# Attention inside an adaLN block: short diagonal units merged, and the softmax denominators summed wholly on GpSimd

## The chip, the cores and the metric

The kernel runs on one core of one Trainium2 chip. The metric is the device time of one execution in microseconds (us). Three runs of the kernel before gave 1782.09, 1782.79 and 1783.23 us; their median, 1782.79 us, is the time to compare with.

## What is computed

The reference is one transformer block with adaptive layer norm on a sequence `x` of 2048 rows of 1024 features, all in float32. A modulation vector gives six rows `sa, ca, ga, sb, cb, gb`. Cut to what matters here:

```python
h = layernorm(x) * (1 + ca) + sa
q, k, v = h @ Wq, h @ Wk, h @ Wv          # 32 query heads of 32 features, 8 key/value heads
q, k = rope(q), rope(k)
scores = q @ k.T / sqrt(32)               # each of the 8 k heads serves 4 query heads
scores = where(column > row, -huge, scores)   # causal mask, 2048 x 2048 per head
x = x + ga * ((softmax(scores) @ v) @ Wo)
h = layernorm(x) * (1 + cb) + sb
x = x + gb * lora_experts(h)              # top 1 of 8 experts, each of rank 16
```

The change touches only the attention: the row maxima of the scores, the weights `exp(score - max)`, and their sums (the softmax denominators).

## The kernel before

**Steps.** The attention is done in 32 steps `n = (qb, m)`: query block `qb` of 512 rows (four of them) times a group `m` of four query heads (eight of them). A step of block `qb` has `nk = 4 * (qb + 1)` key tiles of 128 keys: 4, 8, 12 or 16. The last four key tiles of a step lie on the diagonal; key tile `kc` there needs only the queries from `offset(kc) = kc * 128 - qb * 512` on, so that the four have 512, 384, 256 and 128 columns.

**Visits.** TensorE holds a step's work in *visits*. The letters are those of the order that is described below.

- **M, maxima** (`maxima_units`, 320 visits before). For 128 query rows `t` of the block and 512 keys `kc`, four matmuls that run side by side in the four row groups of the array (32 rows each, one per head) write four PSUM banks `sm` (L1426). On the diagonal (`kc == qb`) only `(t + 1) * 128` columns exist, and 16 small bf16 matmuls from the tables `pick` and `later` (L1419) write the mask first. VectorE then takes one maximum per bank (L1432). When a step's last unit is done, `split_maxima` (L1441 to L1447) turns the maxima into three bf16 parts on GpSimd.
- **R, rows** (`shift_rows`, L1454, L1457). The negated maxima are turned into rows `nt`.
- **S, scores** (`Attend.weights`, 320 visits before). For one key tile, again in the four row groups and in four PSUM banks `sc`: the negated maxima by a bf16 matmul (L1479), the mask on the diagonal (L1487, 16 matmuls), the scores (L1492). ScalarE takes the exponential of each bank into the tile `et` (L1498), 128 keys by four heads by 512 queries. There are four `et` buffers.
- **P, sums** (`weighted_sum`, L1508). Four matmuls, in the four *column* groups of the array, add `et` times `v` into one bank `po`. Right after each, `accumulate` (L1524, L1526) adds `et` to the running sum `acc` in SBUF: on GpSimd, and in the last of the 32 steps on VectorE. It covers all key tiles but the last two.
- **D, shares** (`denominators`, L1534). Four column-group matmuls with a matrix of ones sum `acc` over its 128 partitions into the bank `pd`, and eight more do so for the last two key tiles, taken straight from their `et` buffers. ScalarE copies `pd` (L1539), VectorE inverts it in four parts (L1543), GpSimd multiplies (L1547).
- **F and T, everything else** on TensorE: the projections (`pq`, `pk`, `pv`), the output product (`pw`), the second half of the block (`tr_c`, `pa`, `pwh`, `pf`). They are column-group or full-array matmuls.

A visit of kind M or S is in *row form* here, P, D, R and most of F in *column form*.

**What sets the order.** `plan_order` searches, before anything is issued, for an order of all visits. It keeps a list of states, each with the clock that it imagines for each engine, with when each PSUM bank (eight), each `et` buffer and the running sum become free, and with prices in us written into it: a change of form between visits (`start`), 0.00875 us per column for GpSimd's additions, and so on. Each state is ranked by TensorE's idle time so far and by how far maxima and other work are from the pace that they should have. The maxima run about one step ahead of the scores. The order found is then issued as it is; the engines wait for one another only by semaphores. At most two key tiles are scored and not yet summed, the third key tile of a step is not scored before D of the step before, and `acc` is not begun again before that D.

**Start and end.** The first 125 us or so project the first 512 rows. The last 47 us (`finale`) have the last step's D, its part of the output product, and the second half of the last 512 rows.

The functions that the change touches, and what calls them, with the profile's line numbers:

Of the kernel before, what the change touches and what calls it, by code (L numbers as in the profile page):

```python
# [10 lines left out]
F32 = mybir.dt.float32  # L11
# [85 lines left out]
def plan_order(parts, trail, steps, ahead, starts, tiles, ends, rates, gates):  # L97
# [87 lines left out]
    def maxima(s):  # L185
        n, t, kc = ahead[s[MAXIMA]]
        qb = steps[n][0]
        nk = QB if kc < qb else (t + 1) * P
        masked = kc == qb
        ready, turned = take(s, 4), unit_needs[s[MAXIMA]][1]  # L190
        if turned:
            ready = max(ready, s[TURNED][turned - 1] + TO_PE)
        s[PE] = start(s, "Rb" if masked else "R", ready) + 0.00167 * nk + (0.15 if masked else 0.0)
        s[WORK] += 0.00167 * nk
        after = s[PE] + TO_ENGINE
        give(s, *[(use(s, DVE, 0.07 + 0.00104 * nk, after) + TO_PE, b) for b in s[GOT]])
        s[MAXIMA] += 1
        if s[MAXIMA] - 1 == final[n]:
            done = use(s, POOL, 1.3, use(s, DVE, 0.15, 0.0) + BETWEEN)
            s[MINUS] = s[MINUS] + (done + TO_PE,)  # L200
# [10 lines left out]
    def scores(s):  # L211
        n, kc = tiles[s[SCORED]]
        if kc == 0:
            s[NOW] = n
            flush(s)
        width = QB - max(0, kc * P - steps[n][0] * QB)
        s[PE] = start(s, "Rb", max(take(s, 4), s[MINUS][n])) + 0.00209 * width
        s[WORK] += 0.00209 * width
        if kc >= 4 * steps[n][0]:
            s[PE] += 0.13  # L220
        free, s[ETS] = s[ETS][0], s[ETS][1:]
        after = max(s[PE] + TO_ENGINE, free)
        read = []
        for b in s[GOT]:
            done = use(s, ACT, 0.07 + 0.00083 * width, after)
            read.append((done + TO_PE, b))
        give(s, *read)
        s[READY] = s[READY][1:] + (done,)
        s[CREDIT] += rates[s[SCORED]]
        s[SCORED] += 1  # L230
# [4 lines left out]
    def sums(s):  # L235
        i = s[SUMMED]
        n, kc = tiles[i]
        nk = 4 * (steps[n][0] + 1)
        width = QB - max(0, kc * P - steps[n][0] * QB)
        ready = et_ready(s, i)  # L240
        at = ready + TO_PE
        if kc == 0:
            at = max(at, take(s, 1))
            s[SUM_BANK] = s[GOT][0]
        s[PE] = start(s, "C", at) + 0.00167 * width
        s[WORK] += 0.00167 * width
        if kc == nk - 1:
            give(s, (use(s, ACT, 0.5, s[PE] + TO_ENGINE) + TO_PE, s[SUM_BANK]))
        adder, us = (DVE, 0.0043) if n == last_step else (POOL, 0.00875)
        if kc == 1:  # L250
            s[ACC] = use(s, adder, us * QB, max(ready + BETWEEN, s[ACC_FREE]))
            free_et(s, max(s[ACC], s[PE]), 2)
        elif 1 < kc < nk - 2:
            s[ACC] = use(s, adder, us * width, ready + BETWEEN)
            free_et(s, max(s[ACC], s[PE]), 1)
        s[SUMMED] += 1

    def shares(s):
        flush(s)
        n = s[SHARED]  # L260
        ready = max(take(s, 1), s[ACC] + TO_PE, et_ready(s, ends[n] - 1) + TO_PE)
        s[PE] = start(s, "C", ready) + 0.00167 * (QB + 384)
        s[WORK] += 0.00167 * (QB + 384)
        s[ACC_FREE] = s[PE] + TO_ENGINE
        free_et(s, s[PE], 2)
        s[RD] = use(s, ACT, 0.5, s[PE] + TO_ENGINE)
        give(s, (s[RD] + TO_PE, s[GOT][0]))
        s[LATER] = 5
        s[SHARED] += 1
# [57 lines left out]
    def choices(s):  # L327
# [10 lines left out]
        if s[SCORED] < len(tiles):  # L338
            n, kc = tiles[s[SCORED]]
            if n < s[ROWS] and s[SCORED] - s[SUMMED] < 2 and not (s[SHARED] < n and kc > 1):  # L340
                found.append((max(four, s[MINUS][n] - 0.8), "S", scores))
        if s[SUMMED] < s[SCORED]:
            n, kc = tiles[s[SUMMED]]
            if not (s[SHARED] < n and kc == 1) and s[FILL] >= sums_need[s[SUMMED] > 0]:
                found.append((et_ready(s, s[SUMMED]) + TO_PE, "P", sums))
# [22 lines left out]
    for n, kc in tiles:  # L368
        span = starts[n + 2] - starts[n + 1] if n < last_step else 0.0
        due.append(starts[n + 1] + span * (kc + LEAD) / (4 * (steps[n][0] + 1)))  # L370
# [93 lines left out]
def adaln_block_kernel(  # L464
# [937 lines left out]
    def maxima_units(n):  # L1402
# [3 lines left out]
        def unit(t, kc):  # L1406
            nk = QB if kc < qb else (t + 1) * P
# [5 lines left out]
            ps = score_banks(f"sm_{n}_{t}_{kc}")  # L1413

            if masked:
                for s in range(4):
                    o = t * P + s * HD
                    for j, rows in groups:
                        nc.tensor.matmul(  # L1419
                            ps[j][:, o : o + HD], later[rows, s, :],  # L1420
                            pick[rows, s, s * HD : (s + 1) * HD], start=(s == 0), stop=False,
                        )
            spans = [(t * P, nk), (0, t * P)] if masked and t else [(0, nk)]
            for a, b in spans:
                for j, rows in groups:
                    nc.tensor.matmul(  # L1426
                        ps[j][:, a:b], q[rows, t * P : (t + 1) * P],
                        k[rows, kc * QB + a : kc * QB + b], start=not masked,
                        stop=(a, b) == spans[-1],
                    )  # L1430
            for j in range(4):
                nc.vector.tensor_reduce(mx[:, t, j : j + 1, kc], ps[j][:, :nk], AX.X, ALU.max)  # L1432

        units = [lambda t=t, kc=kc: unit(t, kc) for t in range(4) for kc in range(qb + 1)]
        return units

# [22 lines left out]
    class Attend:  # L1459
        def __init__(self, n):  # L1460
            self.n = n
            self.qb, self.m = steps[n]
            self.nk = 4 * (self.qb + 1)
            self.ets = {}

            last = n == len(steps) - 1
            self.adder = nc.vector if last else nc.gpsimd
# [4 lines left out]
        def weights(self, kc):  # L1472

            off, qb = self.offset(kc), self.qb
            q, k, nt = quad(self.m, qb), k_t[:, self.m // 4, :], nts[self.n % 2]
            ps = score_banks(f"sc_{self.n}_{kc}")

            for j, rows in groups:
                nc.tensor.matmul(  # L1479
                    ps[j][:, off:], ones_h[rows, :], nt[rows, off:],  # L1480
                    start=True, stop=False,
                )
            if kc >= 4 * qb:
                for s in range(4):
                    w = (s + 1) * HD
                    for j, rows in groups:
                        nc.tensor.matmul(  # L1487
                            ps[j][:, off : off + w],
                            pick[rows, s, :], later[rows, s, :w], start=False, stop=False,
                        )  # L1490
            for j, rows in groups:
                nc.tensor.matmul(  # L1492
                    ps[j][:, off:], k[rows, kc * P : (kc + 1) * P], q[rows, off:],
                    start=False, stop=True,
                )
            et = epool.tile([P, 4, QB], F32, tag="et", name=f"et_{self.n}_{kc}")
            for j in range(4):
                nc.scalar.activation(  # L1498
                    et[:, j, off:], ps[j][:, off:], AF.Exp, scale=1.0 / math.sqrt(HD)
                )  # L1500
            self.ets[kc] = et

        def weighted_sum(self, kc):
            off, et = self.offset(kc), self.ets[kc]
            if kc == 0:
                self.po = bank(f"po_{self.n}")
            for j, rows in groups:
# [3 lines left out]
                    start=(kc == 0), stop=(kc == self.nk - 1),  # L1511
                )
            if kc == self.nk - 1:
                nc.scalar.copy(quad(self.m, self.qb), self.po)

        def accumulate(self, kc):

            off, et = self.offset(kc), self.ets[kc]
            if kc == 1:
# [5 lines left out]
            elif 1 < kc < self.nk - 2:  # L1525
                self.adder.tensor_add(self.acc[:, :, off:], self.acc[:, :, off:], et[:, :, off:])  # L1526

        def denominators(self):
            pd = bank(f"pd_{self.n}")
            parts = [(0, self.acc)]  # L1530
            parts += [(self.offset(kc), self.ets[kc]) for kc in (self.nk - 2, self.nk - 1)]
            for i, (off, et) in enumerate(parts):
                for j, rows in groups:
                    nc.tensor.matmul(  # L1534
                        pd[rows, off:], ones_p[:, :HD], et[:, j, off:],
                        start=(i == 0), stop=(i == 2),
# [20 lines left out]
    for n, (qb, m) in enumerate(steps):  # L1557
        ahead += [(n, t, kc) for t in range(4) for kc in range(qb + 1)]
# [7 lines left out]
    tiles = [(n, kc) for n in range(len(steps)) for kc in range(4 * (steps[n][0] + 1))]  # L1566
    attend = [Attend(n) for n in range(len(steps))]
    ends = [sum(s.nk for s in attend[: n + 1]) for n in range(len(steps))]
# [23 lines left out]
    for n, t, kc in ahead:  # L1592
        qb, m = steps[n]
        b = 2 * qb + t // 2
# [13 lines left out]
        parts, [k for k, _ in trail], steps, ahead, starts, tiles, ends, rates, gates  # L1608
# [5 lines left out]
    for letter, banks in order:  # L1614
# [15 lines left out]
        elif letter == "S":  # L1630
            n, kc = tiles[i]
            now[0] = n
            attend[n].weights(kc)
        elif letter == "P":
            n, kc = tiles[i]
# [68 lines left out]
```

## Time and profile before

| | value |
|---|---|
| median of three runs | 1782.79 us |
| the profiled execution's own time | 1782.16 us |
| its span, first to last instruction | 1780.4 us |
| granted TensorE clock, mean | 0.996 |
| VectorE busy | 1094.3 us, 61% of the span |
| ScalarE busy | 740.0 us, 42% |
| maxima on VectorE (L1432) | 1280 instructions, 689.0 us |
| exponentials on ScalarE (L1498) | 1280 instructions, 578.4 us |
| additions to `acc` on GpSimd (L1526, 180 instructions, and L1524, 31) | 792.8 and 132.1 us |

TensorE's share in four stretches that are cut where a block's last D begins: 200.1 of 204 us (block 0, from 125 us on), 324.3 of 327 us (block 1), 503.2 of 507 us (block 2) and 568.8 of 570 us (block 3).

How to read the rows: "PE" is a matmul, "PEld" the load of its weights, which may lie under the matmul before. A float32 matmul shows as two records, so that "x8" stands for four matmuls. Matmul ends are modelled and overlap what follows, so the length of a visit is read here from its start to the next visit's start. "32*128" is a row-form matmul (32 rows of the array, 128 columns), "128*32" a column-form one.

### The profile page before, as it was taken

The page shows a single profiled execution, that of the slowest core. Times are in us where ns is not written, and L with a number is a line of the kernel's source. Part 1 is how long each engine was busy: PE and PEld are TensorE (multiplying, and loading weights), DVE is VectorE, ACT ScalarE, POOL GpSimd, SP SyncE. Part 2 cuts the span into 40 slices and gives each one's busy share as a digit, 9 for nine tenths or more (in the row PEclk, how much of TensorE's full clock was granted, in tenths as well). Part 3 has the DMA queues.
Part 4 walks back from the last instruction along what each step waited for, and adds up shares of the span by engine and source line. Part 5 has one row for each costly group of instructions (what it writes and reads, how often), then busy time and mean ns, then how long its engine had stood idle before and what let it go on. Part 6 is the DMA issues. An engine that isn't in the chain of part 4 may idle for free.

```text
span 1780.4 us, 55951 instructions
## 1 busy us (share of the span) xinstructions
PE 1747.0 (98%) x25112; PEld 708.9 (40%) x25112; DVE 1094.3 (61%) x2160; ACT 740.0 (42%) x1634; POOL 1185.1 (67%) x568
## 2 busy tenths in 40 slices
PE   7999999999999999999999999999999999999997
PEld 3655555444444333334444343333333333333333
DVE  2455456755755674676475566575566765666497
ACT  1203334344433424455444333454544444455452
POOL 1233343487567649657885866978979778798852
PEclk9999999999999999999999999999999999999999
DMA  9512323212422421131103011101102111110101
GB/s 350 181 30 74 115 80 103 73 50 62 137 73 96 153 87 49 49 102 61 61 26 125 26 49 68 41 37 49 49 25 73 37 61 49 49 49 25 49 13 49
DMA packets 68496, 130.57 MB, mean 73 GB/s; under 512 B 3744, under 2 KB 20768, under 8 KB 68256
## 3 DMA queue, kind: packets, MB, share of 16 engines
q1 hardware_dynamic: 66928, 125.85, 20.5%
q8 instruction: 196, 3.21, 0.8%
q10 hardware_dynamic: 1328, 1.15, 0.2%
q14 instruction: 44, 0.36, 0.1%
HBM read 118.59 MB, written 8.39 MB: 71 GB/s over the span
## 4 chain that ended last, share of the span: by engine, by line
PE 88%; POOL 6%; DVE 2%; issue 2%; DMA 1%; ACT 1%; POOLq 0%; ACTq 0%; DVEq 0%
PE sm L1426 15%; PE po L1508 14%; PE sc L1492 12%; PE pw L675 11%; PE pq L966 11%; PE sc L1479 5%; POOL acc L1526 5%; PE pd L1534 3%; PE pk L675 3%; PE pv L675 2%; PE pa L675 2%; PE open L966 2%; PE pf L675 2%; PE sm L1419 1%; DVE mx L1432 1%
## 5 line engine op out<-in xcount | busy, mean ns | idle before, releaser
L1432 DVE TENSOR_REDUCE mx<-sm 128x1 f32<-128x512 f32 (+3 forms) x1280 | 689.0, 602 | 397.7 <-PE sm L1426 396.2
L1498 ACT ACTIVATE et<-sc 128x512 f32<-128x512 f32 (+3 forms) x1280 | 578.4, 540 | 705.5 <-PE sc L1492 701.3
L1526 POOL TENSOR_TENSOR acc<-acc,et 128x2048 f32<-128x2048 f32 (+1 forms) x180 | 792.8, 4404 | 31.8 <-ACT et L1498 22.8
L1426 PE MATMUL sm<-k_t,q 32*128 32x512 f32 (+3 forms) x3328 | 336.6, 475 | 3.0 <-ACT et L1498 3.0
L1492 PE MATMUL sc<-q,k_t 32*128 32x512 f32 (+3 forms) x2560 | 297.2, 536 | 0.0
L1508 PE MATMUL po<-et,v_sb 128*32 128x512 f32 (+3 forms) x2560 | 294.8, 538 | 0.1
L675 PE MATMUL pw<-w,q 128*32 128x512 f32 x1920 | 238.7, 598 | 0.0
L1524 POOL TENSOR_TENSOR acc<-et,et 128x2048 f32<-128x2048 f32 (+1 forms) x31 | 132.1, 4261 | 98.5 <-ACT et L1498 83.1
L966 PE MATMUL pq<-h_t,w 128*32 128x256 f32 x3072 | 191.9, 384 | 0.0
L1426 PEld LDWEIGHTS sm<-k_t,q 32*128 32x128 f32 x3328 | 139.5, 184 | 116.9 <-issue 43.5
L966 PEld LDWEIGHTS pq<-h_t,w 128*32 128x32 f32 x3072 | 90.5, 110 | 100.6 <-issue 44.8
L1508 PEld LDWEIGHTS po<-et,v_sb 128*32 128x32 f32 x2560 | 59.0, 108 | 175.5 <-issue 152.3
L1543 DVE RECIPROCAL rd<-rd 128x128 f32<-128x128 f32 x128 | 112.4, 919 | 18.9 <-ACT rd L1539 18.8
L1479 PE MATMUL sc<-nt,ones_h 32*128 32x512 bf16 (+3 forms) x1280 | 120.1, 352 | 3.5 <-ACT rd L1539 2.9
L1112 POOL TENSOR_TENSOR x<-ag,x 128x512 f32<-128x512 f32 x40 | 60.9, 1523 | 87.3 <-DVE ag L1111 87.3
L1492 PEld LDWEIGHTS sc<-q,k_t 32*128 32x128 f32 x2560 | 115.5, 185 | 5.8 <-issue 2.1
L1479 PEld LDWEIGHTS <-ones_h 32*128 32x128 bf16 x1280 | 32.9, 91 | 207.6 <-issue 201.5
L844 POOL TENSOR_TENSOR swap_q<-swap_q,cs 128x512 f32<-128x512 f32 x32 | 40.9, 1277 | 105.7 <-DVE swap_q L841 105.7
L675 PEld LDWEIGHTS pw<-w,q 128*32 128x32 f32 x1920 | 50.1, 109 | 129.3 <-issue 110.8
L1547 POOL TENSOR_TENSOR q<-q,rd 128x512 f32<-128x512 f32 x31 | 41.6, 1343 | 67.3 <-DVE rd L1543 49.5
L1111 DVE TENSOR_TENSOR ag<-pw,gate 128x512 f32<-128x512 f32 x40 | 27.5, 687 | 62.5 <-PE pw L675 60.9
L844 POOL TENSOR_TENSOR swap_k<-swap_k,cs 128x512 f32<-128x512 f32 x8 | 10.2, 1276 | 82.7 <-DVE swap_k L841 82.7
(146 smaller groups left out, 1340.0 us busy)
## 6 DMA issues: line engine op xcount, KB each, us to landing
w<-in_wo_dram SPq DMA_DIRECT2D x112, 256.0 KB
w<-in_wmod_dram SPq DMA_DIRECT2D x48, 512.0 KB
w<-in_wq_dram SPq DMA_DIRECT2D x48, 512.0 KB
x<-in_x_dram SPq DMA_DIRECT2D x32, 512.0 KB
out_dram<-x SPq DMA_DIRECT2D x16, 512.0 KB
w<-in_wv_dram SPq DMA_DIRECT2D x12, 512.0 KB
w<-in_wk_dram SPq DMA_DIRECT2D x12, 512.0 KB
wq<-in_wq_dram SPq DMA_DIRECT2D x8, 512.0 KB
```

The lines of the kernel that those rows point to most:

```text
L675: nc.tensor.matmul(dst[rows], left[:, rows], right, start=start, stop=stop)
L966: nc.tensor.matmul(ps[j * HD : (j + 1) * HD, a * TB : (a + 1) * TB], self.query_weights(half, k, j * P + h * HD), self.h_t[:, k, :], start ...
L1112: nc.gpsimd.tensor_add(x1[t][:, cols], tmp, x1[t][:, cols])
L1426: nc.tensor.matmul(ps[j][:, a:b], q[rows, t * P : (t + 1) * P], k[rows, kc * QB + a : kc * QB + b], start=not masked, stop=(a, b) == spans ...
L1432: nc.vector.tensor_reduce(mx[:, t, j : j + 1, kc], ps[j][:, :nk], AX.X, ALU.max)
L1479: nc.tensor.matmul(ps[j][:, off:], ones_h[rows, :], nt[rows, off:], start=True, stop=False,)
L1492: nc.tensor.matmul(ps[j][:, off:], k[rows, kc * P : (kc + 1) * P], q[rows, off:], start=False, stop=True,)
L1498: nc.scalar.activation(et[:, j, off:], ps[j][:, off:], AF.Exp, scale=1.0 / math.sqrt(HD))
L1508: nc.tensor.matmul(self.po[rows, off:], v_sb[:, kc, 4 * (self.m // 4) + j, :], et[:, j, off:], start=(kc == 0), stop=(kc == self.nk - 1),)
L1524: self.adder.tensor_add(self.acc[:, :, off:], first[:, :, off:], et[:, :, off:])
L1526: self.adder.tensor_add(self.acc[:, :, off:], self.acc[:, :, off:], et[:, :, off:])
L1543: nc.vector.reciprocal(part, part)
```

## The change

Three things change, and the planner is told of each.

1. In the maxima of steps from the third on, the diagonal units of `t = 0` (128 columns) and `t = 2` (384 columns) are one visit in one set of four banks (`unit_list`). The two units' matmuls and VectorE's two maxima per bank stay as many as they were.
2. In the scores, the key tiles of a step are taken in the order ..., nk-3, nk-1, nk-2. Tiles nk-3 (384 columns) and nk-1 (128 columns) are one visit in one set of four banks; it takes two `et` buffers at once.
3. GpSimd adds the last two key tiles to `acc` too, so that D has only the four matmuls over `acc`. The last step keeps D as it was.

```diff
+    def unit_list(n):
+
+        qb = steps[n][0]
+        if n < 2:
+            return [((t,), 0) for t in range(4)]
+        out = []
+        for t in range(4):
+            out += [((t,), kc) for kc in range(qb)]
+            out += [((), ((1,), qb), ((0, 2), qb), ((3,), qb))[t]] if t else []
+        return out
...
             for j in range(4):
-                nc.vector.tensor_reduce(mx[:, t, j : j + 1, kc], ps[j][:, :nk], AX.X, ALU.max)
...
+                for t, a, b in runs:
+                    nc.vector.tensor_reduce(mx[:, t, j : j + 1, kc], ps[j][:, a:b], AX.X, ALU.max)
...
+            self.order = [*range(self.nk - 2), self.nk - 1, self.nk - 2]
+            self.packs = [[kc] for kc in self.order]
+            self.packs[-3:-1] = [self.order[-3:-1]]
...
+            self.apart = 2 if last else 0
...
             for j in range(4):
-                nc.scalar.activation(
-                    et[:, j, off:], ps[j][:, off:], AF.Exp, scale=1.0 / math.sqrt(HD)
-                )
...
+                for kc, off, a, b in runs:
+                    nc.scalar.activation(
+                        self.ets[kc][:, j, off:], ps[j][:, a:b], AF.Exp, scale=1.0 / math.sqrt(HD)
+                    )
...
-            elif 1 < kc < self.nk - 2:
+            elif 1 < i < self.nk - self.apart:
                 self.adder.tensor_add(self.acc[:, :, off:], self.acc[:, :, off:], et[:, :, off:])
...
         def denominators(self):
             pd = bank(f"pd_{self.n}")
             parts = [(0, self.acc)]
-            parts += [(self.offset(kc), self.ets[kc]) for kc in (self.nk - 2, self.nk - 1)]
+            apart = self.order[self.nk - self.apart :]
+            parts += [(self.offset(kc), self.ets[kc]) for kc in apart]
             for i, (off, et) in enumerate(parts):
                 for j, rows in groups:
                     nc.tensor.matmul(
                         pd[rows, off:], ones_p[:, :HD], et[:, j, off:],
-                        start=(i == 0), stop=(i == 2),
+                        start=(i == 0), stop=(i == self.apart),
                     )
```

In the planner, D now waits for `acc` alone, and the buffers of the last two tiles come free when GpSimd has added them, not when D has read them:

```diff
-        elif 1 < kc < nk - 2:
+        elif 1 < kc < (nk - 2 if n == last_step else nk):
             s[ACC] = use(s, adder, us * width, ready + BETWEEN)
             free_et(s, max(s[ACC], s[PE]), 1)
...
-        ready = max(take(s, 1), s[ACC] + TO_PE, et_ready(s, ends[n] - 1) + TO_PE)
-        s[PE] = start(s, "C", ready) + 0.00167 * (QB + 384)
-        s[WORK] += 0.00167 * (QB + 384)
+        s[PE] = start(s, "C", max(take(s, 1), s[ACC] + TO_PE)) + 0.00167 * QB
+        s[WORK] += 0.00167 * QB
         s[ACC_FREE] = s[PE] + TO_ENGINE
-        free_et(s, s[PE], 2)
```

Since the planner searches anew, the whole issue order differs from the third step on.

## The prediction

> **What bounds the kernel now.** I read the page first. TensorE is busy almost throughout, and the chain that ended last is 88% TensorE. GpSimd has 6% of that chain, which needs a closer look, since the change gives it more to do.
>
> ```profile
> span 1780.4 us, 55951 instructions
> PE 1747.0 (98%) x25112; PEld 708.9 (40%) x25112; DVE 1094.3 (61%) x2160; ACT 740.0 (42%) x1634; POOL 1185.1 (67%) x568
> PE   7999999999999999999999999999999999999997
> POOL 1233343487567649657885866978979778798852
> PE 88%; POOL 6%; DVE 2%; issue 2%; DMA 1%; ACT 1%; POOLq 0%; ACTq 0%; DVEq 0%
> ```
>
> Second, who waits for GpSimd's sum: the answer for the tile `acc` has only one waiting line on TensorE's side, 1.8 us in all. Its 6% of the chain is a path that runs beside busy TensorE, not a stall.
>
> ```profile
>   PEld pd L1534: 1.8, 3
> ```
>
> Third, the windows. In block 3 TensorE has 1.2 us without work out of 570, and GpSimd 468 us of work: 82%, its fullest stretch.
>
> ```profile
> 1163.00:1733.00 570.00, 568.81 (x6684) 192.20 (x6680) 372.94 (x661) 281.25 (x598) 467.63 (x161) 1.00 0.12 43
> ```
>
> So time is gained by taking work or form changes off TensorE, and by hardly anything else. Fourth, the timeline of TensorE, for the price of a change of form. The first column is the start; I take a visit from its start to the next one's.
>
> ```profile
> 1147.84 1.06 PE L675 MATMUL pw<-w,q 128*32 128x512 f32 x8
> 1148.84 0.23 PE L1479 MATMUL sc<-nt,ones_h 32*128 32x128 bf16 x4
> ...
> 1151.95 1.04 PE L675 MATMUL pw<-w,q 128*32 128x512 f32 x8
> 1152.81 0.40 PE L1508 MATMUL po<-et,v_sb 128*32 128x128 f32 x8
> ...
> 1160.96 1.03 PE L1492 MATMUL sc<-q,k_t 32*128 32x512 f32 x8
> 1161.82 1.03 PE L1426 MATMUL sm<-k_t,q 32*128 32x512 f32 x8
> 1162.77 1.07 PE L1534 MATMUL pd<-acc,ones_p 128*32 128x512 f32 x8
> 1163.66 0.83 PE L1534 MATMUL pd<-et,ones_p 128*32 128x256 f32 x16
> 1164.42 0.40 PE L1479 MATMUL sc<-nt,ones_h 32*128 32x512 bf16 x4
> ...
> 1182.28 1.03 PE L1492 MATMUL sc<-q,k_t 32*128 32x512 f32 x8
> 1183.24 0.66 PE L742 MATMUL tr_c<-ident,xn 128*128 128x128 f32 x4
> ```
>
> The same four output matmuls take 1.00 us ahead of a row-form visit and 0.86 ahead of another column visit: 0.14 for going in. With `po` it is 1.00 against 0.88 (medians of the whole timeline), with `pq` 0.55 against 0.45. I take 0.12. The scores' four matmuls take 0.86 ahead of another row visit and 0.96 ahead of a full-array one: 0.10 for going out. A run of row-form visits costs 0.22 us beside its own work.
>
> **The change part by part.**
>
> **D without the two last tiles** (31 of 32 steps). The line `pd<-et`, x16, goes from 1163.66 to 1164.42, 0.76 us; 0.12 of that is the change of form, which the matmuls over `acc` pay instead. 0.64 x 31 = 19.8 us of TensorE, all on its path. ScalarE's copy and VectorE's inversions stay.
>
> **Shared visits.** 30 maxima and 32 score visits go. Their matmuls, masks, maxima and exponentials stay, so the gain is the change of form alone, and only where the neighbours are column work. I counted that in both programs' issue orders: before, 320 + 320 visits lie in 588 runs of row form; after, 290 + 288 in 535. 53 x 0.22 = 11.7 us. The rest of the new order pays nothing else: what full-array work adds and loses in changes is under ten in number.
>
> Here the Trainium skill is weighed. *TensorEngine Tiling (Array Packing)*, Key Properties, says that a change of tiling mode drains TensorE; *TensorE: Matmul & The Clock Gate*, Single matmul latency, puts the constant part of a lone matmul at about 175 ns. If each change cost that (an estimate from these pages), a run would cost 0.35 and the 53 runs 18.6 us. The rows have 0.10 to 0.14, so I keep 11.7; 18.6 is the far end.
>
> A shared visit keeps its banks until both halves are done: a bank's first reader starts after the last matmul of the second half, some 0.4 us later. In return a set of four banks is asked for 62 times less. Maxima of 512 columns between column visits have a median of 1.07 us but a mean of 1.11, so bank waits are some 0.04 us each, 13 us over 320; a tenth fewer visits may save 1. I take 1, between -2 (all waits grow by a sixth) and 3.
>
> **GpSimd.** It gains an addition of 4 x 128 and one of 4 x 256 in 31 steps. Its rows: 2048 elements 4541 ns, 1536 elements 3455 ns, 512 elements 1272 to 1343 ns. 1024 lies between: 2.37 us. 1.28 + 2.37 = 3.65 us a step, 113 us in all, 1185 to 1298. In block 3, seven steps are GpSimd's: 468 + 26 = 493 of some 560 us, 88%. That is still cover, but at the handover from one step to the next it is a new wait: D now waits for the additions of the last tiles, and behind D wait the third tile of the next step and the start of its sum. Behind the additions themselves, in GpSimd's own queue, wait the split of the maxima, the rotary products and the additions to `x`.
>
> What is it worth? The handover in the fence above: GpSimd ended its last addition at 1156.1, and D began at 1162.8. All 31 handovers, read so: 20 had more than 3.65 us between, the other eleven fall short by 16 us together. That is the cost if TensorE keeps its old order and stands idle for each shortfall. The new order puts work there: from the scores of the last tile to D, TensorE has 4 to 21 us of other visits (their columns at the rates above), in block 3 from 7 to 17. A sum that is up to date needs 4 x 0.389 us of exponentials, 1.28 and 2.37: 5.2 us. One that is also behind by tile nk-3 needs 8.7. Six to eight steps have less than that, by some 20 us in all. So 0 to 20 us; I take 3, near the lower end, since the row nearest to it (waits of D for `acc`) is 1.8 us today, with an order made the same way. It cannot be below zero: no wait goes away by it.
>
> Again a rule stands against it: *GPSIMD Engine Reference*, Engine selection, would have such additions on VectorE, at half the time. The rows agree on the ratio (VectorE 2.69 us for 2048 elements in the last step), and the pair would take about 1.9 us a step in place of 3.65. By the rule 31 x 1.8 = 54 us are given away. By the windows they are on no path as long as TensorE has work to put in: 0 to 20.
>
> **The two `et` buffers at once.** Of four, a shared visit takes two, and the last tiles' buffers come free after GpSimd, not after D. This holds up scores, not TensorE, while maxima and projections are there; it is in the 0 to 20.
>
> **Sum.** Against the profiled execution, 1782.2 us: - 19.8 - 11.7 - 1 + 3 = 1752.7. The median of the runs is 0.6 above that execution, so 1753 us, 1.7% less. Start (125 us) and end (47 us) have none of this.
>
> **The rivals.**
>
> *GpSimd becomes the bound at the handovers* (5%, the slower side). One mechanism: in blocks 2 and 3 GpSimd is a full addition behind when the last tile comes, and TensorE has used up what it may do before D, so that each of 15 steps waits a full 4.5 us: 68 us, 1753 - 3 + 68 = 1818. It turns into a loss from 31.5 / 15 = 2.1 us a step on. For it: block 3's 88%, and 4 to 5 us of GpSimd standing idle for the next sum to begin at a handover (1162.98 to 1167.90), which a later D makes longer. Against it: 1.8 us of such waits today at 82%, and 7 to 17 us of cover.
>
> *Part of that* (14%): 1 us at most handovers, 15 to 25 us: 1765 to 1775.
>
> *The shared visits don't pay* (10%): later release of banks and buffers makes the maxima wait as much as the 53 changes save. Only D's part remains: 1782.8 - 19.8 = 1763. For it: the 0.04 us of waits per maxima visit; against: the same reads in the same number, on engines at 61% and 42%.
>
> *More than that* (6%): a change of form is worth the 0.35 us of the rule, or waits shrink too: 1753 - 7 - 3 = 1743 or less.
>
> **How the numbers follow.** The likeliest case, 1747 to 1760, has 65%. The range goes from 1744 to 1769: below it lies most of the last rival, above it half of the partial one and the slower one, together under 2 in 10. A difference of 0.2%, 3.6 us, is about what these runs can tell from none. Faster by more than that: 0.94, all cases but the slower one and a thin edge of the partial one; the same 0.02; slower 0.04.
>
> **What would show it.** In the changed profile: no `pd<-et` but the last step's eight matmuls; TensorE's busy time near 1717; GpSimd near 1298, with rows of 512 and 1024 elements at about 1.3 and 2.4 us; waits of `pd` for `acc` of 2 to 6 us; TensorE in block 3 with fewer than 5 us idle. I am wrong if `pd` waits for `acc` by 20 us or more, if `sm` and `sc` visits are longer than their columns say, or if the split of the maxima comes so late behind the additions that `nt` (0.6 us of waits today) holds TensorE.

## The result and the profile after

The changed kernel takes 1755.97 us (median of 4 runs, 1754.85 to 1757.38) against 1782.44 for the kernel before: ratio 0.9853, 95% interval 0.9839 to 0.9868. That is 26 us less; 1753 was forecast. The profile's page after, with the rows that answer to those of before:

```profile
span 1752.6 us, 55165 instructions
PE 1716.0 (98%) x24616; PEld 704.6 (40%) x24616; DVE 1089.0 (62%) x2160; ACT 737.9 (42%) x1634; POOL 1297.5 (74%) x630
PE   7999999999999999999999999999999999999997
POOL 1235646578878775869786989789889899898952
PE 77%; POOL 15%; DVE 2%; issue 2%; ACT 1%; DMA 1%; SPq 0%; POOLq 0%; ACTq 0%; DVEq 0%
```

TensorE has 31 us less of work (1747.0 to 1716.0) and GpSimd 112 us more. GpSimd's share of the chain has risen from 6 to 15%. The rows of GpSimd's new additions, by shape (mean ns of one after the bar), and TensorE's waits for `acc`, `nt` and `rd`:

```profile
L1571 POOL TENSOR_TENSOR acc<-acc,et 128x1024 f32<-128x1024 f32 x31 | 73.3, 2365 | 5.8 <-ACT et L1543 4.0
L1571 POOL TENSOR_TENSOR acc<-acc,et 128x512 f32<-128x512 f32 x31 | 39.5, 1273 | 2.1
```

```profile
PE nt L1484 <- POOL nb L1477: 3.2, 4, 1.2
PE sm L1445 <- ACT rd L1585: 3.0, 1, 3.0
PE pd L1580 <- POOL acc L1571: 2.9, 5, 1.2
```

One shared visit of each kind in the timeline: the maxima of `t` = 0 and 2 first, the key tiles nk-3 and nk-1 second (a row names only its first shape; the 128 columns of nk-1 are among the x8 and x16).

```profile
1038.78 0.37 PE L1432 MATMUL sm<-pick,later 32*128 32x32 bf16 x32
1038.99 1.19 PE L1445 MATMUL sm<-k_t,q 32*128 32x128 f32 x24
1040.11 1.07 PE L975 MATMUL pq<-h_t,w 128*32 128x256 f32 x16
...
1058.46 0.40 PE L1521 MATMUL sc<-nt,ones_h 32*128 32x384 bf16 x8
1058.69 0.47 PE L1529 MATMUL sc<-later,pick 32*128 32x32 bf16 x32
1058.99 1.09 PE L1535 MATMUL sc<-q,k_t 32*128 32x384 f32 x16
1060.01 1.92 PE L684 MATMUL pw<-w,q 128*32 128x512 f32 x16
```

The first takes 1.33 us, where two visits took 0.51 and 0.95; the second 1.55, where two took 1.12 and 0.59 (medians of the timelines). With the 0.12 us of going in that one of the two no longer pays, a shared visit between column work saves 0.25 and 0.28 us.

### The profile page after: what moved, and what is told of

Same layout as the page of the kernel before. It is cut to its first block, busy times and chain, and to the rows that moved or that the text cites. A ratio compares the mean times of both kernels' runs of the same rounds, so it can differ in the third digit from the quotient of the medians.

```text
span 1752.6 us, 55165 instructions
## 1 busy us (share of the span) xinstructions
PE 1716.0 (98%) x24616; PEld 704.6 (40%) x24616; DVE 1089.0 (62%) x2160; ACT 737.9 (42%) x1634; POOL 1297.5 (74%) x630
## 4 chain that ended last, share of the span: by engine, by line
PE 77%; POOL 15%; DVE 2%; issue 2%; ACT 1%; DMA 1%; SPq 0%; POOLq 0%; ACTq 0%; DVEq 0%
POOL acc L1571 14%; PE sm L1445 13%; PE po L1553 12%; PE sc L1535 11%; PE pq L975 11%; PE pw L684 10%; PE sc L1521 4%; PE pk L684 3%; PE pv L684 2%; PE pd L1580 2%; PE open L975 2%; PE mr L790 1%; PE pf L684 1%; DVE mx L1452 1%; PE pa L684 1%
## 5 line engine op out<-in xcount | busy, mean ns | idle before, releaser
L1571 POOL TENSOR_TENSOR acc<-acc,et 128x2048 f32<-128x2048 f32 (+1 forms) x242 | 905.1, 3740 | 28.1 <-ACT et L1543 14.8
L1535 PE MATMUL sc<-q,k_t 32*128 32x512 f32 (+3 forms) x2560 | 291.0, 533 | 0.0
L975 PE MATMUL pq<-h_t,w 128*32 128x256 f32 x3072 | 187.9, 382 | 0.0
L1521 PE MATMUL sc<-nt,ones_h 32*128 32x512 bf16 (+3 forms) x1280 | 115.2, 351 | 1.8 <-DVE mx L1452 1.0
```

What stands on the lines that cost most here:

```text
L975: nc.tensor.matmul(ps[j * HD : (j + 1) * HD, a * TB : (a + 1) * TB], self.query_weights(half, k, j * P + h * HD), self.h_t[:, k, :], start ...
L1521: nc.tensor.matmul(ps[j][:, a:b], ones_h[rows, :], nt[rows, off:], start=(kc == kcs[0]), stop=False,)
L1535: nc.tensor.matmul(ps[j][:, a:b], k[rows, kc * P : (kc + 1) * P], q[rows, off:], start=False, stop=(kc == kcs[-1]),)
```

## The experiments

Each was timed in five rounds against the kernel before on the same chip. Gains in us are the ratio times 1782.5; the intervals are about 2.5 us wide to either side. Theory A is the prediction's price list with small waits. Theory C is the prediction's far end for a change of form, 0.35 us a pair, which it worked out from the two pages that it names. The other rivals are named in the expectations.

**1. GpSimd's sums alone.**

```diff
-            self.order = [*range(self.nk - 2), self.nk - 1, self.nk - 2]
+            self.order = [*range(self.nk)]
-            self.packs[-3:-1] = [self.order[-3:-1]]
...
+        return [((t,), kc) for t in range(4) for kc in range(steps[n][0] + 1)]
```

> GpSimd sums all key tiles, but no visit is shared. Theory A (the price list: 0.64 us of TensorE per D, 0.22 us per run of row-form visits, waits of a few us): D gives 19.8 us; this program's order has 598 runs of row form against 588 before, which costs 2.2; with 3 us of waits for the sum: 1782 - 15 = 1767. Theory B (the handovers to GpSimd give much of D's gain back, 1 us or more in most of the 31): 1775 to 1790. If the result is A's, waits of D's matmuls for acc stay under 6 us.

1763.24 us, ratio 0.9893 (0.9880 to 0.9907): 19 us less, somewhat more than A and far from B. `pd` waited 2.9 us for `acc`. The handover to GpSimd does not eat D's gain.

**2. The shared maxima alone.** The scores as in experiment 1, the planner's and the kernel's D as before, with `unit_list` of the change.

```diff
-        elif 1 < kc < (nk - 2 if n == last_step else nk):
+        elif 1 < kc < nk - 2:
...
-            self.apart = 2 if last else 0
+            self.apart = 2
```

> Only the maxima's diagonal units of t = 0 and t = 2 share a visit; scores and D are as before. Theory A: 570 runs of row form against 588, 18 x 0.22 = 4.0 us less: 1778. Theory C (a change of form costs the 0.35 us a pair that a drain of 175 ns each would give): 18 x 0.35 = 6.3: 1776. Theory D (banks held longer eat it): 1782 or more.

1780.74 us, ratio 0.9992 (0.9983 to 1.0000): 1.4 us less, below A. But the banks were not the reason: cut from start to start, the timeline has 323 us of `sm` here against 338 before. The gain was lost elsewhere, in part on waits such as these of the projections (`pv`) and of the modulation (`mc`):

```profile
PE pv L686 <- ACT h_t L740: 5.8, 3, 4.6
PE mc L804 <- DVE rows L798: 5.5, 7, 1.0
PE mc L816 <- DVE rows L798: 2.5, 1, 2.5
```

The change has no hand in these but through the order that the planner found. That order has a fault besides: it makes the rows `nt` of step 4 at 196.15 us, in the buffer that step 2 still needs for its last key tile, which is scored at 200.38. Nothing in the planner forbids this, so the output of this program is wrong (relative error 0.048), though none of its work is missing. So this run tells nothing on the price of a shared visit, and gave reason to look at the order itself.

**3. The shared scores alone.** As experiment 2, with the scores of the change and the maxima of before.

```diff
+        return [((t,), kc) for t in range(4) for kc in range(steps[n][0] + 1)]
```

> Only the key tiles nk-3 and nk-1 share a score visit; maxima and D are as before. Theory A: 557 runs of row form against 588, 31 x 0.22 = 6.8 us less: 1775.5. Theory C (0.35 us a pair): 10.9 less: 1771.5. Theory D (two et buffers at once and banks held longer eat it): 1782 or more.

1773.64 us, ratio 0.9949 (0.9936 to 0.9961): 9 us less, between A and C. D falls: taking two `et` buffers at once holds nothing up that shows.

**4. Both shared visits, D as before.** Only the edit of `apart` and of the planner's prices that experiment 2 shows.

> Both kinds of shared visit, D as before with its eight extra matmuls. Theory A: 536 runs of row form against 588, 52 x 0.22 = 11.4 us less: 1771. Theory C: 18.2 less: 1764. Theory D: 1780 or more. Theory B needs this run to be near 1771 and the changed kernel to gain far less than 19.8 us on top of it; A has the changed kernel at this run's time minus 19.8 plus 3.

1765.66 us, ratio 0.9907 (0.9893 to 0.9920): 16.6 us less, again between A and C. Now there was a riddle. The sums alone are worth 19 us and the visits alone 16.6, 36 together, and the change that has both is worth 26. Two explanations were left: D's part is worth less beside the shared visits, or the order of the changed kernel is poor.

**5. D's matmuls put back as dead work**, in the changed kernel's own order.

```diff
+            if not self.apart:
+                for off in (QB - 2 * P, QB - P):
+                    for j, rows in groups:
+                        nc.tensor.matmul(
+                            pd[rows, off:], ones_p[:, :HD], self.acc[:, j, off:],
+                            start=(off == QB - 2 * P), stop=(off == QB - P),
+                        )
             for i, (off, et) in enumerate(parts):
```

> The changed kernel in its own order, to the instruction, with D's eight matmuls put back as dead work (over 256 and 128 columns of acc, overwritten by the real ones) in the 31 steps that lost them; the planner isn't told. It prices D's part in place, free of any other order. Theory A (0.64 us each on TensorE's path): 1756 + 19.8 = 1776. Theory E (D stands at a place where TensorE waits anyway, so its matmuls were partly free): 1762 to 1770. The shared visits alone (1766) lie only 10 us above the changed kernel, which is what E would give; under A the missing 10 us are waits that came in with the new order.

1775.14 us, ratio 0.9956 (0.9944 to 0.9969): 18.4 us above the changed kernel by the ratios, 19.2 by the medians. A holds and E falls. In the timeline of this run the dead part goes from 1142.05 to 1142.72, 0.67 us, where 0.64 was forecast:

```profile
1142.05 0.86 PE L1581 MATMUL pd<-acc,ones_p 128*32 128x256 f32 x16
1142.72 1.04 PE L1587 MATMUL pd<-acc,ones_p 128*32 128x512 f32 x8
1143.58 1.90 PE L684 MATMUL pw<-w,q 128*32 128x512 f32 x16
```

**6 and 7. One dead matmul in each shared visit**, of column form and, as the control, of row form. It stands between the matmuls of the two halves, in maxima and scores alike; `none` holds zeros.

```diff
+        nc.tensor.matmul(ps[0][:HD, 0:1], none[:, :HD], ones_p[:, 0:1], start=False, stop=False)
```

```diff
+        nc.tensor.matmul(ps[0][:, 0:1], none[:HD, :], ones_p[:HD, 0:1], start=False, stop=False)
```

> The changed kernel in its own order, with one dead column-form matmul of one column (it adds zero) between the halves of each of the 62 shared visits, so that form changes twice more in each. Against the next kernel, which has a row-form one there: theory A (0.22 us a pair): 13.6 us more than it. Theory C (two drains of 175 ns): 21.7 more. Theory F (the gain was not from form changes): within 4 us of it.

> The control of the kernel before it: the same place, one dead row-form matmul of one column, no change of form. All theories: the bare cost of one small matmul and its weight load, 0.05 to 0.25 us each, so 1759 to 1771.

1776.44 us (ratio 0.9961, 0.9949 to 0.9974) and 1766.42 us (0.9911, 0.9898 to 0.9925). The column one costs 9 to 10 us more than the control, about 0.15 us a visit: A's 13.6 was too high, C's 21.7 out of reach, F (within 4) too low. Column form first, control second, the same kind of visit:

```profile
1129.35 0.37 PE L1434 MATMUL sm<-pick,later 32*128 32x32 bf16 x32
1129.56 0.53 PE L1449 MATMUL sm<-k_t,q 32*128 32x128 f32 x8
1130.02 0.22 PE L1447 MATMUL sm<-ones_p,none 128*32 128x1 f32 x2
1130.17 0.94 PE L1449 MATMUL sm<-k_t,q 32*128 32x128 f32 x16
1131.04 0.64 PE L1559 MATMUL po<-et,v_sb 128*32 128x256 f32 x8
```

```profile
1186.18 0.37 PE L1434 MATMUL sm<-pick,later 32*128 32x32 bf16 x32
1186.40 0.53 PE L1449 MATMUL sm<-k_t,q 32*128 32x128 f32 x8
1186.70 0.28 PE L1447 MATMUL sm<-ones_p,none 32*128 32x1 f32 x2
1186.74 1.01 PE L1449 MATMUL sm<-k_t,q 32*128 32x128 f32 x16
1187.67 1.92 PE L686 MATMUL pw<-w,q 128*32 128x512 f32 x16
```

1.69 and 1.49 us, against 1.33 without either. Going out and in is visible: the column one starts 0.46 us after the matmuls ahead of it, the row one 0.30. But the two small matmuls differ in more than form: the control loads 128 columns of weights, the column one 32, and such loads take about 0.18 and 0.11 us in these traces. So 0.15 us is rather too low for a pair, and 0.36 (1.69 less 1.33), which has the small matmul in it, too high. The 0.25 and 0.28 of the visits themselves lie between.

**8. The same work with a wider search.**

```diff
-    WIDTH, GRAIN = 200, 0.4
+    WIDTH, GRAIN = 600, 0.4
```

> The changed kernel's work with a planner that keeps 600 states in place of 200: the same matmuls in another order (544 runs of row form against 535). It shows how much of any difference between two plans is the order found. Theory A (the price list, waits alike): 9 x 0.22 = 2 us more, 1758. Theory G (the order found matters by many us, and the sums that don't add up are this): more than 5 us from 1758 on either side.

1742.55 us, ratio 0.9779 (0.9765 to 0.9792): 13 us faster than the changed kernel with the very same matmuls, and with more runs of row form, 539 against 535 (counted in the trace; the expectation's 544 is too many, and 4 x 0.22 us would be 1 us). G holds. It is the fastest kernel of this study.

```profile
span 1738.0 us, 55149 instructions
PE 1708.2 (98%) x24616; PEld 701.4 (40%) x24616; DVE 1089.1 (63%) x2160; ACT 737.7 (42%) x1634; POOL 1299.7 (75%) x630
```

**9 and 10. The wider search for the kernel before, and for the shared visits with D as before.** The same edit in each.

> The kernel before with a planner that keeps 600 states in place of 200 (589 runs of row form against 588). Theory G (the order found matters by many us, for any of these kernels): clearly below 1782, some 1765 to 1776, and the change is then worth 1742.5 minus this under a like search. Theory H (only the changed kernel was unlucky with 200 states; the order before was about as good as it gets): 1778 to 1784, and the change is worth 40 us, more than its price list of 31.5 by what the waits shrink.

> Both kinds of shared visit, D as before, 600 states (533 runs of row form). Theory A with like orders: the changed kernel with 600 states (1742.5) plus D's 19.8 less 3 of waits: 1759, so that the parts add up. Theory B (GpSimd's additions give much of D's part back even with a better order): 1755 or less.

1776.39 us (ratio 0.9963, 0.9951 to 0.9976) and 1765.41 us (0.9901, 0.9888 to 0.9915). The kernel before gains 6.6 us by the search, the changed kernel 13, experiment 4's nothing clear (1 us). Neither G (whose changed kernel was only one of many) nor H has it quite: both orders had something to gain, the changed kernel's twice as much. With 600 states in all three, the visits are worth 11.0 us (0.9963 - 0.9901; A with 56 runs fewer, 589 against 533: 12.3) and the sums on top of them 21.7 (0.9901 - 0.9779), each give or take some 3.5. For the sums A had 19.8 less 3 of waits: experiment 10 lies 6 us above the 1759 expected, on the side away from B. It is 32.8 in all, where the prediction had 31.5 ahead of waits. That the two parts make up the whole is so by construction, since the second is measured on top of the first; what speaks for the list is that the visits are near their price, and the sums no lower than theirs. The sums alone were not run with 600 states.

**11. The two short additions on VectorE**, 600 states, the planner told.

```diff
             elif 1 < i < self.nk - self.apart:
-                self.adder.tensor_add(self.acc[:, :, off:], self.acc[:, :, off:], et[:, :, off:])
+                adder = nc.vector if i >= self.nk - 2 else self.adder
+                adder.tensor_add(self.acc[:, :, off:], self.acc[:, :, off:], et[:, :, off:])
```

> The changed kernel with 600 states, and the additions of the last two key tiles on VectorE in place of GpSimd; the planner is told. The rule that such additions belong on VectorE has the sum ready earlier by up to 1.8 us a step. Theory A (they lie beside other work on either engine): 1742.5 within 5. Theory B (GpSimd's handover is what TensorE waits for): 5 to 15 less, 1728 to 1737. Against it: VectorE's additions wait for GpSimd's and stand ahead of maxima in VectorE's queue, which frees banks later: above 1748.

1755.18 us, ratio 0.9849 (0.9834 to 0.9864): 12.5 us slower than experiment 8. The rule that the prediction weighs, such additions on VectorE, found no support here. The two do take less time there, 1.34 and 0.78 us in place of 2.37 and 1.27. But VectorE's busy time rises by 65 us to 1154.1. TensorE's longest waits that experiment 8 does not have, one of them for the maxima, are:

```profile
PE sc L1523 <- ACT rd L1588: 2.4, 1, 2.4
PE mc L816 <- DVE rows L798: 2.0, 1, 2.0
PE pw L686 <- DVE mx L1454: 1.3, 1, 1.3
```

From start to start, `sc` has 6.5 us more than in experiment 8, `sm` 3.9, `po` 2.9. How much of it is the order found once more can't be told: orders differed by 7 to 13 us above. This order also has experiment 2's fault (the `nt` of steps 5 and 6 come before the last key tiles of steps 3 and 4), so that its output is wrong (relative error 0.106). B, a gain of 5 to 15 us, finds no support; that VectorE is the worse engine for these additions is not shown.

**12. The sum made late.** The changed kernel's own order, 200 states.

```diff
             elif 1 < i < self.nk - self.apart:
+                if i == self.nk - 1:
+                    nc.gpsimd.tensor_copy(self.acc, self.acc)
```

> The changed kernel in its own order (200 states), with a copy of acc onto itself on GpSimd ahead of the last addition of each of the 31 steps, some 2 to 2.5 us; the planner isn't told. Theory A in the form of the prediction (4 to 21 us of other visits lie ahead of D): most of it hidden, 1756 to 1775. Theory I (the planner puts D where the sum is just ready, so that nothing is left over): each delay reaches TensorE almost whole, 31 x 2.3 = 70 us more, 1815 to 1830.

1788.05 us, ratio 1.0030 (1.0018 to 1.0041): 32 us above the changed kernel. The copy takes less than assumed, 1.89 us, 58.6 in all, so that 55% of it shows in the time. Both theories miss. The wait is where it was looked for, 2.9 us before:

```profile
PE pd L1582 <- POOL acc L1573: 28.2, 20, 3.1
```

```profile
L1572 POOL COPY acc<-acc 128x2048 f32<-128x2048 f32 x31 | 58.6, 1890 | 1.6
```

In 20 of 31 steps D now stands still for it, and the changed kernel's trace says which. A step in it, GpSimd's last additions (they end at 563.16) and D:

```profile
555.91 7.25 POOL L1571 TENSOR_TENSOR acc<-acc,et 128x1536 f32<-128x1536 f32 x3
563.21 1.07 PE L1580 MATMUL pd<-acc,ones_p 128*32 128x512 f32 x8 [0.16 <-POOL acc L1571]
```

The same step with the copy:

```profile
568.77 1.37 PE L1582 MATMUL pd<-acc,ones_p 128*32 128x512 f32 x8 [2.07 <-POOL acc L1573]
```

From the end of the last addition to D there are 0.05 us here. Read so in all steps, 20 of 31 have less than 1.89 us (in the kernel before 5; its median is 4.2 us, here 1.3), and they lack 26.0 us of it in all; the waits rose by 25.3, in these same 20 steps. So the planner did put D right behind the additions that it knew of, as theory I has it, but in 20 steps, not in all.

The two profiled executions lie 34.6 us apart (1787.2 and 1752.6), and the rest of that is TensorE's clock. In this trace it is granted at half for 27 us, in seven stretches, each of which begins close to the end of such a wait (from 0.4 us before it to 1.4 behind it); in the changed kernel's for 6.8 us (and its last 1.7). Half of the difference, some 10 us, is lost. All six runs of this program have a lower mean clock (0.991 to 0.994) than the four of the changed kernel (0.996 to 0.998). Not every wait of that length is followed by such a stretch. One of them:

```profile
569.40:572.82 3.42, 3.42 (x18) 0.72 (x16) 0.65 (x3) 0.58 (x1) 3.34 (x3) 0.50 0.14 55
570.08 2.09 PE L1445 MATMUL sm<-k_t,q 32*128 32x512 f32 x8
572.10 1.39 PE L1553 MATMUL po<-et,v_sb 128*32 128x512 f32 x8
```

The 0.50 is the granted clock; the maxima visit takes 2.02 us, where its median is 1.07.

## Why the prediction was right, point by point

**What bounds the kernel: right.** TensorE is busy for 98% of both spans.

**D's part, 19.8 us: right.** 18.4 to 19.2 in place (experiment 5), 21.7 under a like search (10 and 8). The changed profile has only the last step's eight matmuls of `pd` over `et` (16 records of them).

**The shared visits, 11.7 us: right in size.** A pair of changes was taken as 0.22 us; the visits' own rows say 0.25 and 0.28. The runs gave 16.6 us with 200 states where the list has 11.4, and 11.0 with 600 where it has 12.3. The far end, 0.35 us a pair, would be 19.6 for those 56 runs, which is not what a like search shows, and for the dead matmuls (6 and 7) its 21.7 was more than twice the 9 to 10 measured. (The 16.6 alone would have fitted it; that was the order.) That a change of form costs time stands; the price is the row's.

**GpSimd, 3 us of waits: right in kind.** Its rows of 2.365 and 1.273 us are the 2.37 and 1.28 that were taken between rows of other shapes, its busy time of 1297.5 the 1298. TensorE's matmuls of `pd` waited 2.9 us for `acc` (2 to 6 foretold; none is listed for the kernel before). The 1.8 us that the prediction went by were waits of the weight loads, and on that count it is now 10.5, which for the most part lie under other matmuls:

```profile
  PEld pd L1580: 10.5, 11
```

`nt`, named as a danger, waits 3.2 in place of 0.6, but not for the additions: experiment 4, without them, has the same 3.2, and experiment 1, with them, 0.6.

What the prediction had wrong is the cover: it gave 4 to 21 us of visits ahead of D as room, while 1.89 us more a step already reached TensorE in 20 of 31 steps (12). (Its count of handovers in the kernel before is also a little off: 19 have more than 3.65 us, and the other twelve fall short by 19 us, not eleven by 16.) This was not needed for the time, but the rival that GpSimd becomes the bound was nearer than 5% made it look: 1.89 us more a step, if the planner isn't told of it, turned a gain of 26 us into a loss of 5.

**What the sum lacked: the order itself.** The list and its 3 us of waits missed by 3 us, and that is chance: the order found weighs more. Block 3 was to have less than 5 us without TensorE work and has 3.8 (581 us from D of step 23 to D of step 31; it isn't quite the work of the 570 us before, 6715 matmuls against 6684):

```profile
1126.00:1707.00 581.00, 577.24 (x6715) 192.07 (x6711) 384.21 (x690) 281.57 (x599) 498.46 (x183) 1.00 0.12 44
```

Most waits are spread, about 1 us each at most, behind a visit. From the timeline of TensorE, cut from start to start and summed by kind (us), and the span less its busy time:

| | before | changed | before, 600 | changed, 600 |
|---|---|---|---|---|
| `sm` | 337.6 | 337.0 | 331.2 | 328.6 |
| `sc` | 358.6 | 353.1 | 356.6 | 352.5 |
| `pd` | 53.8 | 31.4 | 53.2 | 30.8 |
| without work | 33.4 | 36.6 | 30.9 | 29.8 |

`pd` has its 22 us in both pairs. But `sm`, with 30 visits fewer, is no shorter in the changed kernel: its shared visits save some 4 us by their own length (30 x 0.13), but what its maxima visits have beyond the medians of their shapes is 28 us, where the kernel before has 24. With the wider search that is 19 and 18, and `sm` is 2.6 us shorter than in the kernel before.

One place stands out in the changed kernel, a wait of 3.0 us inside a maxima visit, and 6.8 us at half the clock right behind it, in which a visit of `po` takes 1.87 us in place of 1.00:

```profile
296.58 1.82 PE L1445 MATMUL sm<-k_t,q 32*128 32x512 f32 x2 [3.05 <-ACT rd L1585]
298.33 1.94 PE L1553 MATMUL po<-et,v_sb 128*32 128x512 f32 x8
296.87:303.69 6.82, 6.82 (x74) 2.23 (x76) 1.86 (x5) 2.48 (x10) 4.64 (x2) 0.50 0.01 2
```

Together that is 6.4 us, half of the 13 that the wider search gains; its trace has no such wait for `rd`, and no stretch at half the clock between its first 13 us and its last 2. The kernel before has such a place too (3.0 us for `et`, then 6.8 us at half the clock from 962.5 us on), so it hardly counts in the 26 us of the change. Of the other waits shown above, the one of `pd` is gone from the list of the wider search, and `nt` stays, at 3.4. Why 200 states end in a poorer order for the changed kernel than for the kernel before was not tried.

## What to carry to other kernels

Price a visit from its start to the next one's start, and a change of form from the same matmuls ahead of one kind of neighbour and the other; such a list came within 3 us of 1756 here, which is less than the order alone can move. Where a search writes the order, two versions differ by their work and by the luck of the search (6.6 and 13 us here, half of the whole effect): test a change with more than one search before its parts are judged, or put the part back as dead work in an unchanged order. Work that lies ahead of a planned wait is not slack, because the planner put it there for the delay that it knew: what more delay costs is read step by step from the gap that is left (26.0 us so, 25.3 measured). And where two versions wait differently, compare the granted clock too.

## What the runs showed that was not expected

- GpSimd copies 128 x 2048 float32 in 1.89 us, and adds two such tiles in 4.54: the sum costs 2.4 times the copy.
- In the last step, where VectorE adds to `acc`, GpSimd's additions to `x` take 2.7 to 3.3 us, where the same instruction takes 1.27 before it, and VectorE's own additions of 2048 elements go up to 3.2 us from 2.2. GpSimd's timeline of the changed kernel, an addition in block 3 and three of the last step:

```profile
1350.89 1.27 POOL L1121 TENSOR_TENSOR x<-ag,x 128x512 f32<-128x512 f32 x1
```

```profile
1673.21 3.25 POOL L1121 TENSOR_TENSOR x<-ag,x 128x512 f32<-128x512 f32 x1 [9.15 <-DVE ag L1120]
1688.25 3.32 POOL L1121 TENSOR_TENSOR x<-ag,x 128x512 f32<-128x512 f32 x1
1694.40 3.24 POOL L1121 TENSOR_TENSOR x<-ag,x 128x512 f32<-128x512 f32 x1 [2.83 <-DVE ag L1120]
```

  The Trainium skill (*SBUF — State Buffer*, Who interferes with whom) has a reason: a VectorE `tensor_tensor` with both inputs in SBUF and a GpSimd read exclude each other. The difference, 2 us, is about one addition of VectorE (2.2 us). No run here tried it by itself, and what it costs this kernel was not measured.
